# Two graph-attention and expert layers on one core: row norms written ahead of the mask step, and rows of x asked for on ScalarE's queue

## The chip, the cores and the metric

The kernel runs on one core of a Trainium2 chip. The metric is device time in microseconds (us). Beside it there is one profiled execution, whose trace gives every instruction of every engine: PE (TensorE, the matrix unit), ACT (ScalarE), DVE (VectorE), POOL (GpSimd) and SP (SyncE, which here does nothing but request transfers). "SPq" and "ACTq" in a row are the sequencers of those engines, and a DMA row there is the time in which the request is issued, not the time of the transfer.

## The reference, cut to what matters

The input is x (2708 rows of 256 float32) and an adjacency matrix adj (2708 x 2708, int32, about 1.2% ones). Four steps follow one another, each added to x:

```python
x = x + gnn0(layernorm(x), adj)      # q,k,v; softmax(q k^T / 16 where adj > 0) v; elu
x = x + ffn0(layernorm(x))           # 8 experts, the best 2 of each row, hidden 1024
x = x + gnn1(layernorm(x), adj)      # additive attention under the same mask
x = x + ffn1(layernorm(x))           # 8 experts, the best 2 of each row, hidden 512
```

Only the first of the four, and of it only the beginning, is touched by the change.

## The kernel before, in words

The 2708 rows are cut into NT = 22 tiles of up to 128 rows (the last has 20), and the queries into six blocks of 512 (the last has 148). `layer0_attention` runs over the blocks `b`, and inside a block over the 22 key tiles `k`. A step `k` of block `b` computes the scores of 512 queries against the 128 keys of tile `k` (`scores`, L586), takes the exponential (ACT, L598), multiplies it by the mask (DVE, L601), and three steps later (`LAG = 3`) `attend` adds the product with the values v to four accumulators (L650).

The first block does more than the others, since the keys and values do not exist yet. At step k of block 0 the tile k + 4 is prepared:

- `norm_begin` (bn_stats L282, bn_aggr L283, one more small DVE operation L284, a power on POOL L288), `norm_end` (L292, gives `xn`);
- `prepare`: two transposes on PE (L305), a copy of the result to `xnT` on ACT (L306), a sum on DVE (L499), the value matmuls on PE (L504, two of them, four passes), a copy to `v` on ACT (L508).

Tiles 0 to 3 are prepared ahead of the loop, tiles 4 to 21 in its steps 0 to 17. A tile of x is loaded by `load_x` (L408, 128 KB, into one of 9 buffers `xin`). Tiles 0 to 8 are asked for at the very start, tiles 9 to 21 in the steps 0 to 12, at step k the tile k + 9. Its buffer is the one that tile k had, which is free when `norm_end` of tile k has read it.

The masks come from adj. `masks_of(b)` is a generator that makes the mask of block `b` in pieces: five loads of 1 MB each (L425, four requests of 256 KB, into one of three buffers `adj`), and for each load four pairs of a comparison (`m_rows`, L446) and a 32x32 transpose (`mT`, L452) on DVE. Load i + 2 is written down right after the first comparison of load i. One `next(first_mask)` is one pair. In block 0 two such generators advance: `first_mask` for block 0 itself (its first three loads and its first four pairs are written ahead of the loop) and `later_mask` for block 1. A load into an `adj` buffer has to wait until the four comparisons of the load that had the buffer before are done.

What sets the order of the work:

- SP runs in the order of the program, everywhere (`tc.manual_schedule(engines={SP})` at the top). A request whose buffer is not free holds all requests behind it.
- In block 0, PE, ACT, DVE and POOL run in an order that a planner wrote down when the kernel was built. It simulates the machine with costs of its own, and of what is ready in its simulation it takes the operation that stands first in the program. On the chip each engine then keeps to that order, whatever arrives earlier or later there.
- From block 1 on (L689), PE, ACT and DVE run in the order of the program.

The other requests of SP in block 0 are `load_apart` (L464, at step 4), the packing of expert weights from a list called `background` (after step 8, on odd steps), and, from step 17, five `load_x` that bring the rows of block 0 back for its residual (these use the same function, with its default queue).

Of the kernel before, what the change touches and what calls it, by code (L numbers as in the profile page):

```python
# [27 lines left out]
NT = (N + P - 1) // P  # L28
ROWS = [min(P, N - t * P) for t in range(NT)]
# [14 lines left out]
def of_tile(rows, t):  # L44

    if t >= KEYS:
        return rows[t * P : t * P + ROWS[t], :]
    b = t // GROUP * BN
    return rows[b : b + BN, :].rearrange("(p j) d -> j p d", j=GROUP)[t % GROUP]
# [57 lines left out]
def adj_ffn_kernel(ctx: ExitStack, tc: tile.TileContext, a: dict, out: bass.AP):  # L107
    nc = tc.nc
# [168 lines left out]
    def norm_stats(src, r):  # L277

        st = small.tile([P, 6], F32, name="ln_st")
        mv = small.tile([P, 2], F32, name="ln_mv")  # L280
        rs = small.tile([P, 2, 2], F32, name="ln_rs")
        nc.vector.bn_stats(st[:r], src)  # L282
        nc.vector.bn_aggr(mv[:r], st[:r])  # L283
        nc.vector.scalar_tensor_tensor(  # L284
            rs[:r, 0], once_twice[:r, 0], mv[:r, 1:2], once_twice[:r, 1],
            op0=ALU.mult, op1=ALU.add,
        )
        nc.gpsimd.tensor_tensor(rs[:r, 1], rs[:r, 0], minus_half[:r], ALU.pow)  # L288
        return mv[:r, 0:1], rs[:r, 1, 0:1], rs[:r, 1, 1:2], rs[:r, 0, 0:1]

    def normed(dst, src, mean, factor):
        return nc.vector.tensor_scalar(dst, src, mean, factor, op0=ALU.subtract, op1=ALU.mult)  # L292
# [91 lines left out]
    def layer0_attention(line):  # L384
        with ExitStack() as scope, ExitStack() as until_last:
# [17 lines left out]
                return pool.tile(shape, dtype, name=f"{name}_last", bufs=bufs)  # L403
            xin = {}

            def load_x(t):
                xin[t] = rows0.tile([P, D], F32, name="xin", bufs=9)
                nc.sync.dma_start(xin[t][: ROWS[t]], of_tile(a["x"], t))  # L408

            def masks_of(b, of):  # L410

# [68 lines left out]
            def norm_begin(t):  # L480
                r, src = ROWS[t], xin.pop(t)
                return t, src, norm_stats(src[:r], r)

            def norm_end(t, src, stats):
                r, (mean, factor, *_) = ROWS[t], stats
                xn = rows.tile([P, D], F32, name="xn", bufs=4)
                normed(xn[:r], src[:r], mean, factor)
                return xn

            def prepare(t, xn):  # L490
                r = ROWS[t]
                at = xnT[:, :, t * P : t * P + r]
                if t < NT - 1:
                    to_columns(at, xn[:r], r)
                else:
                    tail_columns(x_tail, xn)
                    nc.vector.tensor_copy(at, x_tail[:, :, :r])
                    r, at = P, x_tail
                nc.vector.tensor_reduce(  # L499
                    sums_of[:, :, t], xnT[:, :, t * P : t * P + ROWS[t]], AX.X, ALU.add  # L500
                )
                ps = misc.tile([P, GROUP, P], F32, name="misc").rearrange("p g n -> p (g n)")
                for c in range(DC):
                    nc.tensor.matmul(  # L504
                        ps[:r, :D], at[:, c, :], wv[:, c, :],
                        start=(c == 0), stop=(c == DC - 1),
                    )
                nc.scalar.copy(v[:r, t, :D], ps[:r, :D])  # L508
# [3 lines left out]
            if True:  # L512
# [5 lines left out]
                for t in range(2, 9):  # L518
                    load_x(t)

                with tc.manual_schedule(
# [10 lines left out]
                    first_mask = masks_of(0, turned_of)  # L532
# [153 lines left out]
            for b, (b0, nb, ts_) in enumerate(BLOCKS):  # L686
                line.gap = GROUP if b >= last - 1 else GROUP + 1
                if b == 1:
                    order0.enter_context(  # L689
                        tc.manual_schedule(engines={  # L690
                            mybir.EngineType.PE,
                            mybir.EngineType.Activation,
                            mybir.EngineType.DVE,
                        })
                    )
                if b + 1 < len(BLOCKS):
                    turned_of[b + 1] = mask_of(b + 1)
                if b == 0:
                    later_mask = masks_of(1, turned_of)
                    next(later_mask)  # L700
                for k in range(NT):
                    if b == 0:
                        if k + 9 < NT:
                            load_x(k + 9)
                        next(first_mask, None)
                        if k + 4 < NT:
                            prepare(k + 4, norm_end(*norm_begin(k + 4)))

                    j = k - (2 if b == last else NT - 1 - GROUP)
                    if 0 <= j < len(ts_):  # L710
                        load_x(ts_[j])
                    if k == (0 if b == last else GROUP):
                        apart_adj = load_apart(b)
                    if k == NT - 8:
                        apart = compare_apart(*apart_adj)
                    late.append((b, k, scores(b, k, g, apart, mT)))
                    if len(late) > LAG:
                        b_, k_, p = late.pop(0)
                        if k_ == 0:
                            accs = [  # L720
                                ps_acc.tile([P, D + 1], F32, name="acc") for _ in BLOCKS[b_][2]
                            ]
                        attend(b_, k_, p, accs)
                        if k_ == NT - 1:
                            evict(b_, accs, total)
                    if b == 1 and k % 2 == 0:
                        next(folding, None)
                    if b == 0 and k == NT - 1:
                        sums = wide.tile([P, DC], F32, name="sums", bufs=1)
                        nc.vector.tensor_reduce(sums, sums_of, AX.X, ALU.add)  # L730
                        total = all_sum(wide, sums, wv, D, "total0")
                    if b == 0 and k == NT - 4:
                        raw = wide.tile([P, BN // QUARTER, P], I32, name="adj", bufs=3)
                        raw = raw.rearrange("p n e -> p (n e)").bitcast(F32)
                        nc.sync.dma_start(
                            raw, a["L0_ffn_Wr"].rearrange("d e -> (d e)").partition_broadcast(P)
                        )
                        gate_rows(raw)
                    if k == NT - 6 and b + 1 < len(BLOCKS):
                        g_next = queries(b + 1)  # L740
                    if k % 3 == 2 if b == last - 1 else k == 0 or k >= 2:
                        next(later_mask, None)
                    if k == NT - 3:
                        even_later = iter(())
                        if b + 2 < len(BLOCKS):
                            even_later = masks_of(b + 2, turned_of)
                            next(even_later)
                    if b > 0 and k == 2:
                        nc.sync.dma_start(neighbours[b - 1][:], turned_of[b - 1])
                    if background and k % 2 == 1 and b < last and (b > 0 or k > 8):  # L750
                        background.pop(0)()
                    if b > 0:
                        line.step()
                    if b == last and k == LAG:
                        until_last.close()
                    if b == last and k == LAG + 2:
                        n = FULL_AFTER[experts0.early]
                        guess0 = experts0.open(
                            [i * (n // RING) * E // (n + GROUP) for i in range(AHEAD)] + [-1]
                        )  # L760
                        for _ in range(AHEAD):
                            next(guess0)
                        begin0 = experts0.begin()
                    if b == last and LAG + 2 <= k < LAG + 8:
                        next(begin0)
                    if b == last and k in (LAG + 9, LAG + 13, LAG + 18):
                        next(begin0)
                if b == last:
                    nc.sync.dma_start(neighbours[b][:], mT)
                else:  # L770
                    for _ in later_mask:
                        pass
                    later_mask = even_later
                    g, mT = g_next, turned_of[b + 1]
# [1345 lines left out]
```

## Time and profile before

| what | value |
|---|---|
| device time, median of 3 runs | 1191.05 us (1186.0 to 1194.85) |
| the profiled execution: its own time, its span | 1177.48 us, 1175.8 us |
| granted TensorE clock in it, mean | 0.990 |
| PE, DVE, ACT, POOL busy in the span | 1125.0, 647.7, 415.4, 430.3 us |
| 0 to 20 us (weights folded, tiles 0 to 3, queries of block 0): PE busy, DMA share | 14.77 us, 0.96 |
| 20 to 132 us (block 0): PE, DVE, ACT busy, DMA share | 105.59, 64.67, 28.43 us, 0.74 |
| 132 to 212 us (block 1): PE, DVE, ACT busy, DMA share | 80.00, 62.07, 19.60 us, 0.75 |

The span is the time from the first to the last instruction in the trace; the execution's own time lies 1.7 us above it, and the median of the runs without a profile 13.6 us above that. A busy PE in such a table has matmuls in flight; it does not mean that the array starts a pass at every moment, so the starts of successive passes are the better measure of what a stretch of PE work costs. The rows of a timeline are: start, duration, engine, line, operation, out<-in, count, and in brackets the idle time of the engine ahead of it with what ended it.

### The profile page before, as it was taken

What the parts mean: (1) busy time and instruction counts of PE and PEld (TensorE: products, weight loads), DVE (VectorE), ACT (ScalarE), POOL (GpSimd) and SP (SyncE); (2) the same over time, 40 slices, a digit from 0 to 9 for tenths busy, and PEclk for the clock granted to TensorE, in tenths of its full rate; (3) what the DMA queues carried; (4) which work ended last, traced back from release to release, by engine and by line L of the source; (5) the groups of instructions that cost most, each with busy time, mean ns of one, the idle gap of its engine ahead of it and who ended that gap; (6) DMA issues with size and microseconds to landing.
All of it is one profiled execution on the core that took longest, in us unless ns stands there. A gap on an engine that the chain in (4) does not pass through costs nothing. (4 is left out here: it accounts for less than half of the span.)

```text
span 1175.8 us, 20858 instructions
## 1 busy us (share of the span) xinstructions
PE 1125.0 (96%) x6421; PEld 912.2 (78%) x6421; DVE 647.7 (55%) x2405; ACT 415.4 (35%) x1232; POOL 430.3 (37%) x519
## 2 busy tenths in 40 slices
PE   8989999999999999999999999998999998998993
PEld 5665666666666666789999999997899997898992
DVE  5565777786876867643222222222876777622224
ACT  3222222222222222433333333332777673344441
POOL 3001212121212122453434343423754557865552
PEclk9999999999999999999999999999999999999997
DMA  9678676867745658579675936543000517577346
GB/s 224 130 163 211 169 183 167 237 168 181 215 128 149 155 140 317 154 206 262 181 197 151 339 83 187 122 159 86 28 1 33 211 56 238 123 241 231 79 131 229
DMA packets 198661, 195.88 MB, mean 167 GB/s; under 512 B 90939, under 2 KB 181524, under 8 KB 192520
## 3 DMA queue, kind: packets, MB, share of 16 engines
q1 hardware_dynamic: 173242, 118.18, 39.7%
q0 software_dynamic: 24256, 70.81, 19.0%
q10 hardware_dynamic: 1038, 5.40, 1.3%
q8 instruction: 55, 0.90, 0.3%
q14 instruction: 70, 0.57, 0.2%
HBM read 246.19 MB, written 66.15 MB: 266 GB/s over the span
## 5 line engine op out<-in xcount | busy, mean ns | idle before, releaser
L1835 PEld LDWEIGHTS mm<-xe,ring 128*128 128x128 f32 x2192 | 260.6, 194 | 15.8 <-DVE xe L1808 5.8
L1835 PE MATMUL mm<-xe,ring 128*128 128x128 f32 x2192 | 263.9, 278 | 5.5 <-DVE xe L1808 3.9
L1843 ACT ACTIVATE hT<-mm,ring 128x128 f32<-128x128 f32 x548 | 156.6, 369 | 287.6 <-issue 157.2
L1851 PE MATMUL acc<-ring,hT 128*128 128x256 f32 x1096 | 252.1, 380 | 0.0
L1851 PEld LDWEIGHTS acc<-ring,hT 128*128 128x128 f32 x1096 | 201.6, 191 | 24.2 <-issue 0.4
L650 PEld LDWEIGHTS acc<-v,p 128*128 128x128 f32 (+1 forms) x880 | 160.0, 190 | 62.4 <-issue 37.0
L650 PE MATMUL acc<-v,p 128*128 128x257 f32 (+1 forms) x880 | 202.7, 383 | 0.0
L586 PE MATMUL s<-g,xnT 128*128 128x512 f32 x420 | 200.3, 597 | 0.6 <-DVE mT L605 0.6
L1551 POOL DMA_INDIRECT disp<-row,to x88 | 92.0, 1045 | 256.9 <-DVE x L670 125.5
L1857 DVE SCALAR_TENSOR_TENSOR y<-acc,who,bias 128x256 f32<-128x256 f32 x92 | 44.3, 481 | 254.6 <-PE acc L1851 232.9
L288 POOL TENSOR_TENSOR ln_rs<-ln_rs,minus_half 128x2 f32<-128x2 f32 x88 | 68.7, 782 | 172.9 <-DVE ln_rs L284 120.4
L598 ACT ACTIVATE p<-s 128x512 f32<-128x512 f32 x105 | 62.7, 597 | 194.8 <-PE s L586 178.7
L930 PE MATMUL acc<-parts,m 128*128 128x266 f32 x924 | 126.2, 293 | 0.0
L930 PEld LDWEIGHTS acc<-parts,m 128*128 128x128 f32 x924 | 117.1, 185 | 4.1 <-ACT raw L957 0.9
L586 PEld LDWEIGHTS s<-g,xnT 128*128 128x128 f32 x420 | 76.8, 190 | 55.1 <-issue 50.3
L1741 POOL DMA_INDIRECT ring<-L_ffn_packed,weight_row x76 | 80.2, 1055 | 92.4 <-PE acc L1851 61.8
L601 DVE SCALAR_TENSOR_TENSOR p<-p,mT 128x512 f32<-128x512 f32 x100 | 71.0, 710 | 75.3 <-ACT p L598 75.2
L1873 POOL DMA_INDIRECT xd<-y,who x45 | 71.2, 1583 | 111.3 <-DVE xe L1814 50.2
L897 ACT CAST m<-mT 128x512 fp32r<-128x512 fp8e4 (+4 forms) x168 | 71.8, 475 | 9.7 <-PE acc L930 6.3
L1863 POOL DMA_INDIRECT xd<-y,who x47 | 50.3, 1071 | 48.6 <-DVE y L1857 44.8
L272 DVE SCALAR_TENSOR_TENSOR row<-x,wr_rows 128x256 f32<-128x256 f32 x128 | 54.4, 425 | 3.3
L1814 DVE TENSOR_SCALAR xe<-xe_raw,ring 128x128 f32<-128x128 f32 x90 | 27.7, 352 | 40.2 <-DMA ring<-L_ffn_packed,weight_row 39.2
(337 smaller groups left out, 1073.1 us busy)
## 6 DMA issues: line engine op xcount, KB each, us to landing
adj<-in_adj_dram SPq DMA_DIRECT2D x100, 256.0 KB
L_ffn_packed<-in_L_ffn_W_dram SPq DMA_DIRECT2D x32, 512.0 KB
xg<-disp SPq DMA_DIRECT2D x368, 32.0 KB
L_ffn_packed<-in_L_ffn_W_dram SPq DMA_DIRECT2D x32, 256.0 KB
neighbours<-mT SPq DMA_DIRECT2D x5, 1408.0 KB
mT<-neighbours SPq DMA_DIRECT2D x5, 1408.0 KB
ring<-L_ffn_packed SPq DMA_DIRECT2D x3, 2182.0 KB
xin<-in_x_dram SPq DMA_DIRECT2D x42, 128.0 KB
```

Of the source, the lines that this page charges most:

```text
L288: nc.gpsimd.tensor_tensor(rs[:r, 1], rs[:r, 0], minus_half[:r], ALU.pow)
L586: nc.tensor.matmul(ps[:kr, :nb], xnT[:, c, k0 : k0 + kr], g[:, c, :nb], start=(c == 0), stop=(c == DC - 1 and k < KEYS),)
L601: nc.vector.scalar_tensor_tensor(p, p, LARGEST, mask, op0=ALU.min, op1=ALU.mult)
L650: nc.tensor.matmul(accs[j][:r], p[keys, q0 : q0 + r], v[keys, k, :], start=(k == 0), stop=(k == NT - 1),)
L897: nc.scalar.copy(m[:, : q1 - q0], MASKS[b].of_key(mTs[b], k)[:, q0 - b * BN : q1 - b * BN],)
L930: nc.tensor.matmul(acc[:r], masks[t], parts[:, k, i], start=(k == 0 and i == 0), stop=False,)
L1551: nc.gpsimd.indirect_dma_start(disp[:], bass.IndirectOffsetOnAxis(ap=to[:r, j : j + 1], axis=0), rows2[:r, j], None,)
L1741: nc.gpsimd.indirect_dma_start(w, None, packed[:], bass.IndirectOffsetOnAxis(ap=self.weight_row[:, s : s + 1], axis=0), bounds_check=E * P ...
L1835: nc.tensor.matmul(ps[:, i, :], w[:, c * hidden + f * P : c * hidden + (f + 1) * P], xe[:, c, :], start=(c == 0), stop=(c == DC - 1),)
L1843: nc.scalar.activation(hT[:, f, :], ps[:, i, :], AF.Gelu, bias=w[:, b1 + f : b1 + f + 1])
L1851: nc.tensor.matmul(ps, hT[:, f, :], w[:, w2 + f * D : w2 + (f + 1) * D], start=(f == 0), stop=(f == hc - 1),)
L1873: start = nc.gpsimd.indirect_dma_start(xd[:], at, y, None, bounds_check=N - 1, oob_is_err=False, compute_op=ALU.add)
```

## The change

In `load_x` the queue becomes an argument, with SP as its default. In block 0's loop three statements change places: `prepare` (with `norm_begin` and `norm_end` inside) now stands first, the load of tile k + 9 second and on ScalarE's queue, the step of the mask third.

```diff
-            def load_x(t):
+            def load_x(t, queue=nc.sync):
                 xin[t] = rows0.tile([P, D], F32, name="xin", bufs=9)
-                nc.sync.dma_start(xin[t][: ROWS[t]], of_tile(a["x"], t))
+                queue.dma_start(xin[t][: ROWS[t]], of_tile(a["x"], t))
...
                 for k in range(NT):
                     if b == 0:
-                        if k + 9 < NT:
-                            load_x(k + 9)
-                        next(first_mask, None)
                         if k + 4 < NT:
                             prepare(k + 4, norm_end(*norm_begin(k + 4)))
+                        if k + 9 < NT:
+                            load_x(k + 9, nc.scalar)
+                        next(first_mask, None)
```

No operation is added or removed: thirteen requests of 128 KB (the last of 20 KB) go from SP to ACT, and the planner sees another order of the program in block 0.

## The prediction

> **What bounds the kernel now.** I began with the busy time of the engines in stretches. PE is busy for 1125.0 of 1175.8 us, and from 132 us on (block 1) for 80.00 of 80.00 us, so the attention is bound by PE. In block 0 it is not quite. What a step costs when nothing is missing is seen in the timeline of 28 to 45 us:
>
> ```profile
> 38.21 1.88 PE L586 MATMUL s<-g,xnT 128*128 128x512 f32 x4
> ...
> 39.93 1.90 PE L650 MATMUL acc<-v,p 128*128 128x257 f32 x8
> ...
> 41.66 1.88 PE L586 MATMUL s<-g,xnT 128*128 128x512 f32 x4
> ```
>
> Read the starts, not the durations: four score passes take 1.72 us (0.43 each), eight attend passes 1.73 us (0.216 each). In the same way two transposes take 0.21 us and the four value passes of a tile 0.87. Multiplied by the counts that the groups of instructions give for 16.5 to 135.1 us (100 score passes, 168 attend passes, 70 value passes, 16 passes for queries at 0.43, 34 transposes, and 4.7 us of small ones) this is 43.0 + 36.3 + 15.1 + 6.9 + 3.7 + 4.7 = 109.7 us of work in a stretch of 118.6. **PE loses 8.9 us there.** The same rates over block 1 (135.1 to 214.5 us) give 79.8 us of work in 79.4, so the rates are good to half a microsecond and block 1 loses nothing.
>
> Where block 0 loses shows in the waits of PE in 20 to 132 us (total, times, longest):
>
> ```profile
> PE misc L305 <- DVE ln_rs L284: 3.2, 2, 2.2
> PE misc L504 <- ACT xnT L306: 1.8, 4, 0.5
> PE misc L305 <- DVE ln_mv L283: 0.7, 1, 0.7
> PE s L586 <- DVE mT L605: 0.6, 1, 0.6
> ```
>
> Three of the four belong to the preparation of a tile: PE has nothing left but the transposes of a tile that is not normed (3.9 us), or two tiles follow one another so closely that it waits for the copy between transposes and value matmuls (1.8).
>
> Then I asked why tiles are late, in SP's timeline:
>
> ```profile
> 24.07 2.58 SPq L425 DMA_DIRECT2D adj<-in_adj_dram  x4
> 26.69 0.61 SPq L408 DMA_DIRECT2D xin<-in_x_dram  x1
> 35.61 8.83 SPq L425 DMA_DIRECT2D adj<-in_adj_dram  x8
> 44.49 1.09 SPq L408 DMA_DIRECT2D xin<-in_x_dram  x2
> 52.22 2.58 SPq L425 DMA_DIRECT2D adj<-in_adj_dram  x4
> 54.84 1.09 SPq L408 DMA_DIRECT2D xin<-in_x_dram  x2
> 62.76 2.58 SPq L425 DMA_DIRECT2D adj<-in_adj_dram  x4
> 65.39 0.63 SPq L464 DMA_DIRECT2D adj_rest<-in_adj_dram  x1
> 66.06 1.09 SPq L408 DMA_DIRECT2D xin<-in_x_dram  x2
> ```
>
> Tile 9 is asked for at 26.69, tile 10 only at 44.49, because two loads of adj stand between them and wait for a buffer. Each row of x leaves in the shadow of a mask load. And the order of DVE was written by a planner that reckoned with this. Tiles 14 and 15 are requested at 66.06, but their statistics come at 81.12:
>
> ```profile
> 81.12 0.73 DVE L282 BATCH_NORM_STATS2 ln_st<-xin 128x6 f32<-128x256 f32 x2
> ...
> 83.67 0.41 PE L305 MATMUL misc<-ident,xn 128*128 128x128 f32 x2 [2.17 <-DVE ln_rs L284]
> ```
>
> DVE waits for xin only once in the kernel (3.8 us at the very start), so the rows had landed; they stand behind a mask product of step 13 and three comparisons in DVE's order. That is the 2.17 us wait.
>
> **The change part by part.**
>
> *Thirteen requests leave SP.* At the median of 0.43 us (tile xin, L408) SP is spared 13 x 0.43 = 5.6 us. Nothing on PE's path waits for SP's issuing itself, so this alone is worth nothing. The mask loads behind them don't go out 5.6 us earlier either: L425 waits for DVE 21.6 us behind mT L452 and 7.1 behind m_rows L446 in that stretch, that is for a buffer.
>
> *The rows come early.* Tile k + 9 needs only the buffer of tile k. Tiles 0 to 3 are normed by 11.5 us, 4 to 8 by 21, so with a free queue tiles 9 to 17 can be asked for by about 21 us instead of 26.69 to 70, and the last well before 45. Here a rule speaks against the change: the Trainium skill, "DMA: Bandwidth & Descriptors", section "Issuing engines are not separate DMA queues", says that requests from several engines end on the same 16 DMA engines and that a second issuing engine saves only the issue time, usually small. By the rule the gain is those 5.6 us of a sequencer that isn't the bound: 0, and 1191. By SP's rows what is saved isn't issue but the hold of 17.8 us between tile 9 and tile 10. I go by the rows, as the rule leaves out a queue standing at a semaphore. Where it does hold is bandwidth: 13 x 128 KB = 1.7 MB move into a stretch (5 to 30 us) where the DMA share is already 0.9 to 1.25; at the 220 GB/s seen there, loads of adj land up to 7.6 us later. The second load of block 0 is compared from 30.77 us, and by the bytes moved until then it had landed near 19, so that cover holds.
>
> *The norms stand first.* In the planner's order of preference the statistics, the norm and the transposes of tile k + 4 now come ahead of that step's comparison, and their rows are there. PE should find a normed tile at each step and place its transposes between score passes, as at 20 to 31 us, where a whole round of scores and preparation takes 2.94 us for 2.80 of work. I take the 3.9 us of waits for a norm as gone. Of the 1.8 us behind the copy I take half: 0.9. The remaining loss (0.6 behind L605, which is the 3.87 us reduction L262, and about 2.6 of small gaps) stays. Gain: 4.8 us; bounds 0 (the planner makes other gaps) and 8.9.
>
> *The comparisons stand later.* Each pair is 0.42 + 0.42 us on DVE, which is busy 64.67 of 112 us; a pair is put back by at most the operations of one tile, 0.41 + 0.17 + 0.22 + 0.41 + 0.41 = 1.6 us. The first key whose mask could be missed is the first of a load (12, 16). The fourth load of adj is asked for from 35.61 us, and the first mask product that needs it (L601 of step 12) runs at 76.99. Cost 0; if the cover is gone, 1.6 us for each of the two loads.
>
> *Thirteen requests on ACT.* No row of before has ACT asking in this stretch; the nearest are ACT's own ring loads, 0.34 us (L1887), and SP's xin, 0.43. I take 0.43: 5.6 us of ACT, which is busy 28.43 of 112. Queued behind a request are the copies L306 (PE waits for them: 9.1 us of weight loads held in 15 times) and the exponentials (three steps of slack). A request hurts only in the window around a copy, about 0.7 + 0.43 of a 4.6 us step: 5.6 x 0.25 = 1.4, less where the planner puts them into ACT's gaps: I take 0.8. Bounds 0 and 5.6, and 11.7 if each is held as SP's first twelve adj requests were (10.77 us, 0.9 each).
>
> **Sum**: -4.8 + 0.8 = -4.0 us, 1177.48 to 1173.5 for an execution like the profiled one. The runs without a profile lie 13.6 us higher at the median, and I carry the difference over: 1191.05 - 4.0 = **1187.0**. Block 1 and what follows keep their order, PE is all but full up to 461 us, so a gain in block 0 arrives whole.
>
> **The rivals.**
>
> *ScalarE is held by its own requests (slower).* For it: SP's queue shows that a request can stand for 8.8 us; the same page, section "Anatomy of one DMA", has every semaphore wait happen on the issuing sequencer before dispatch, and SP's waits agree (21.6 us behind DVE). On SP nothing but requests stood behind; on ACT the copies and exponentials do. If the order written at build time puts requests where, on the chip, the buffer's norm or an older transfer is late, PE pays. Place: 8 to 45 us. It decides from the point where the holds beside a copy exceed the 4.8 us gained. At 0.9 us each, 11.7; if early rows also make the planner set tiles in a row without scores between (two at 71.33 to 75.08 take 3.75 us for some 3.0 of work, 0.35 a tile), another 13 x 0.35 = 4.5. If no wait is removed either: 1191 + 16 = **1207**; with half of both **1199**. Against it: the buffers in question are free early.
>
> *Hidden anyway.* The planner's order moves the gaps, PE waits for masks instead of norms, and the sum stays: **1191**. For it: the loads of adj keep their order and their buffers, and block 0 needs ten of them, 10.5 MB. Against it: no matmul waits for a mask product now, and weight loads do for 1.0 us only.
>
> *More than the norms.* All 8.9 us go, and the 5.2 us that PE idles in 0 to 20 too: **1177**. Against it: the first 20 us hang on weights and copies that don't change.
>
> **How the numbers follow.** 1% of this kernel is 12 us, about what a measurement can tell from no change. Forecast 0.43, slower 0.33, hidden 0.14, more 0.10. The forecast's own range, 1182 to 1191, lies within 1%. Faster by over 1% (under 1179) needs more than PE's whole loss in block 0: 0.10, the last rival. Slower by over 1% (over 1203) gets two thirds of the first rival, 0.22, since an order rewritten by a planner has no firm bound from the profile; the rest, 0.68, is within 1%. The range, 1180 to 1207, holds the forecast, the hidden case and the first rival up to its full price, and leaves out the last and what lies above.
>
> **What would show it.** Right: xin requests of tiles 9 to 17 on ACTq before 25 us; the wait of PE L305 for ln_rs gone; block 1 beginning some 4 us earlier; the same PE counts. Wrong: ACTq rows of several us, PE L504 waiting more behind xnT, or PE L650 waiting for DVE p: then order or masks, not rows, set block 0.

## The result, and the profile after

The changed kernel is a little slower: 1193.45 us (median of 20 runs) against 1188.05 us (20 runs of the kernel before on the same chip), **ratio 1.0047 with an interval of 1.0032 to 1.0062**, some 5.6 us. Forecast were 4 us less. The profiled execution of after has a span of 1192.1 us at a granted clock of 0.984 (before 1175.8 at 0.990), so the ends of these two executions say little about the change. The attention says more: from 212 to 425 us PE is busy for 211.44 us in both, and the difference lies ahead of that.

Three starts on PE locate the loss: the first query pass (L570, end of the prologue), the first pass of the gate (L226, just behind block 0's last attend) and the last query pass of the attention.

| | before | after | difference |
|---|---|---|---|
| first query pass, L570 | 16.6 us | 20.9 us | +4.3 |
| first gate pass, L226 | 132.4 | 136.5 | +4.1 |
| last query pass, L570 | 422.1 | 428.5 | +6.4 |

So 4.3 us are lost ahead of the queries, where the prediction expected nothing, 0.2 are gained in block 0, where it expected 4.0, and 2.3 are lost in block 1, where it expected nothing. Up to the last of these marks PE is granted its full clock in both executions wherever the trace records it.

**Ahead of the queries.** The timeline of after (start, duration, engine, line, operation, count, and in brackets the idle time ahead of it with what ended it), 4 to 12 us:

```profile
4.31 0.80 ACT L545 COPY mT<-misc 128x256 f32<-128x256 f32 x2 [2.23 <-PE misc L544]
...
7.63 0.46 DVE L292 TENSOR_SCALAR xn<-xin,ln_mv,ln_rs 128x256 f32<-128x256 f32 x1
...
8.11 0.39 ACTq L408 DMA_DIRECT2D xin<-in_x_dram  x1
...
8.55 0.65 ACT L545 COPY mT<-misc 128x256 f32<-128x256 f32 x2 [3.44 <-DMA xin<-in_x_dram]
...
8.98 3.36 PE L550 MATMUL s<-mT 128*128 128x256 f32 x7 [3.01 <-ACT mT L545]
```

The four copies L545 belong to the folding of the weights; PE can't go on without them. The planner has set ScalarE's first request of x between the second and the third, and ScalarE stands there from 5.11 to 8.11 us. The request itself takes 0.39 us: what costs is not its row but the idle time in the row behind it. Before, the third copy started at 5.45 us:

```profile
5.45 0.80 ACT L545 COPY mT<-misc 128x256 f32<-128x256 f32 x2 [0.35 <-PE misc L544]
```

Of the 4.3 us the hold itself is 3.1 (the first pass of L550 starts at 8.98 instead of 5.87 us). The other 1.2 is PE's pace: from there to the queries PE takes 11.9 instead of 10.7 us. The trace's record of the clock begins, at full, only at 13.7 us instead of 8.1, and the eight passes L550 start 0.43 us apart after the first, where before they did so up to 8.15 us and then followed at 0.21. Three more requests stand in the prologue, at 9.24, 10.73 and 11.73 us. Each goes out 0.02 to 0.03 us after a norm L292 has let go of its buffer: the norms of tiles 1, 2 and 3 end at 9.21, 10.71 and 11.70 us.

**In block 0** the waits of PE in 20 to 132 us (total, times, longest), to be laid beside those of before:

```profile
PE acc L650 <- DVE p L601: 2.3, 2, 2.0
PE misc L504 <- ACT xnT L306: 1.4, 3, 0.5
PE s L586 <- DVE mT L605: 1.2, 1, 1.2
PE misc L504 <- ACT x_tail L350: 0.7, 1, 0.7
PE misc L570 <- ACT v L508: 0.4, 1, 0.4
```

The waits for a norm are gone, all 3.9 us, as forecast. In their place PE waits for masked scores, for the reduction behind mT and for copies: 6.0 us in all against 6.3. DVE's timeline tells why. Between these two rows it makes, after one mask product, only the norms and sums of tile after tile, and not one comparison:

```profile
37.58 0.42 DVE L446 TENSOR_SCALAR m_rows<-adj 128x512 fp8e4<-128x512 int32 x1
...
65.03 0.75 DVE L446 TENSOR_SCALAR m_rows<-adj 128x512 fp8e4<-128x512 int32 x2
```

By 65 us 20 of the 22 tiles are normed (before: 12), and afterwards PE lives on masks; DVE makes no comparison from 69.9 to 93.3 us either. The attends come in bursts of 32 passes, and at 96.29 us one waits 1.99 us for its mask.

SP is late as well. Its waits in 0 to 60 us have two new lines (before had none for xin there):

```profile
SPq L425 <- DMA xin<-in_x_dram: 14.0, 5, 6.2
SPq L536 <- DMA xin<-in_x_dram: 6.6, 3, 2.9
```

SP asks for adj and constants here, and yet stands until rows of x land; all but 0.9 us of it are rows that ScalarE asked for. The records of the requests tell why (the trace holds them, the views leave this part out). Each request names a semaphore that its transfer raises on landing, and does not go out before the earlier transfer with the same semaphore has landed. SP's and ScalarE's requests share the eight numbers 101 to 108. The request of adj at 24.57 us, for instance, waits for 108 and takes 108; ScalarE's row of 22.39 us had that number before, and SP has stood since 18.33, for 6.2 us, and for the first 4 of them ScalarE had not even asked. It works the other way round too: ScalarE's first request takes 107 from a row that SP asked for at 3.77 us, which landed at 7.66, and only then waits for its norm.

The fourth load of adj goes out at 42.2 instead of 24.1 us. The fifth, at 65.8 instead of 35.6, has stood 21.5 us for the late comparisons and transposes (mT L452).

**In block 1** what stood at the end of SP's queue comes too late:

```profile
131.78 0.59 SPq L214 DMA_DIRECT2D wdst_b<-in_L_gnn_w_att_dram  x1
...
139.39 0.42 DVE L217 SCALAR_TENSOR_TENSOR junk<-wfc,wdst_b 128x256 f32<-128x256 f32 x1 [5.92 <-DMA wdst_b<-in_L_gnn_w_att_dram]
...
141.89 1.57 PE L650 MATMUL acc<-v,p 128*128 128x257 f32 x6 [2.04 <-DVE raw L676]
```

wdst_b, a vector for the second attention's gate, is asked for at 131.8 instead of 108.3 us. From block 1 on DVE keeps the order of the program: its eviction of block 0 (raw, L676) stands behind L217, and PE needs the accumulators that it frees.

### The profile page after: what moved, and what is told of

Same layout as the page of the kernel before. It is cut to its first block, busy times and chain, and to the rows that moved or that the text cites. A ratio compares the mean times of both kernels' runs of the same rounds, so it can differ in the third digit from the quotient of the medians.

```text
span 1192.1 us, 20863 instructions
## 1 busy us (share of the span) xinstructions
PE 1132.3 (95%) x6421; PEld 917.4 (77%) x6421; DVE 643.7 (54%) x2405; ACT 413.1 (35%) x1232; POOL 429.0 (36%) x519
## 5 line engine op out<-in xcount | busy, mean ns | idle before, releaser
L1851 PE MATMUL acc<-ring,hT 128*128 128x256 f32 x1096 | 254.9, 383 | 0.0
L650 PEld LDWEIGHTS acc<-v,p 128*128 128x128 f32 (+1 forms) x880 | 159.9, 190 | 65.6 <-issue 35.8
L650 PE MATMUL acc<-v,p 128*128 128x257 f32 (+1 forms) x880 | 201.9, 383 | 4.3 <-DVE p L601 2.3
L930 PE MATMUL acc<-parts,m 128*128 128x266 f32 x924 | 126.2, 293 | 0.0
L601 DVE SCALAR_TENSOR_TENSOR p<-p,mT 128x512 f32<-128x512 f32 x100 | 68.1, 686 | 46.6 <-ACT p L598 46.5
```

Source lines behind the costliest of these rows:

```text
L601: nc.vector.scalar_tensor_tensor(p, p, LARGEST, mask, op0=ALU.min, op1=ALU.mult)
L650: nc.tensor.matmul(accs[j][:r], p[keys, q0 : q0 + r], v[keys, k, :], start=(k == 0), stop=(k == NT - 1),)
L930: nc.tensor.matmul(acc[:r], masks[t], parts[:, k, i], start=(k == 0 and i == 0), stop=False,)
L1851: nc.tensor.matmul(ps, hT[:, f, :], w[:, w2 + f * D : w2 + (f + 1) * D], start=(f == 0), stop=(f == hc - 1),)
```

## The experiments

All ratios are against the kernel before, run on the same chip, with 95% intervals. The three marks are those above, of one profiled execution each. The last column is the time ahead of the last query for which that execution was granted half the clock; PE moves at half pace there, so at most half of that time is to be taken off the last mark (an estimate).

| run | first query | L226 | last query | ratio | half clock, us |
|---|---|---|---|---|---|
| e1 order only | 16.5 | 132.4 | 422.1 | 1.0002 (0.9989 to 1.0015) | 0 |
| e2 queue only | 19.9 | 135.3 | 428.8 | 1.0064 (1.0041 to 1.0087) | 3.4 |
| e10 one request on ScalarE | 20.0 | 138.8 | 428.5 | 1.0043 (1.0028 to 1.0059) | 6.8 |
| e4 ACT in program order | 17.1 | 132.4 | 426.5 | 1.0011 (0.9997 to 1.0026) | 10.2 |
| e3 rows on GpSimd's queue | 17.2 | 131.9 | 426.9 | 1.0054 (1.0032 to 1.0075) | 3.4 |
| e6 after, wdst_b early | 20.7 | 136.0 | 428.4 | 1.0056 (1.0035 to 1.0076) | 0 |
| e7 e4, wdst_b early | 17.6 | 133.3 | 425.7 | 0.9995 (0.9980 to 1.0010) | 6.8 |
| e9 e7 in the old order | 17.3 | 130.2 | 422.6 | 0.9989 (0.9976 to 1.0003) | 3.4 |
| e14 e7, gate rows early | 16.4 | 130.9 | 421.6 | 0.9991 (0.9979 to 1.0002) | 0 |
| e16 e6, gate rows early | 22.4 | 139.1 | 429.8 | 1.0054 (1.0034 to 1.0074) | 0 |
| e5 four rows ahead on SP | 17.1 | 130.6 | 421.8 | 0.9981 (0.9971 to 0.9992) | 0 |
| e11 e5, wdst_b early | 17.2 | 130.5 | 423.0 | 0.9995 (0.9984 to 1.0006) | 0 |
| e13 e5, mask step first | 16.8 | 131.3 | 422.5 | 1.0006 (0.9990 to 1.0022) | 0 |
| e12 only tiles 9 to 12 early, SP | 17.0 | 139.4 | 429.1 | 1.0044 (1.0029 to 1.0058) | 6.8 |
| e15 e11, gate rows early | 17.0 | 140.7 | 431.4 | 1.0059 (1.0037 to 1.0081) | 10.2 |
| **e17 tiles 9 to 12 on SP, rest on ScalarE** | 17.1 | 126.2 | 415.8 | **0.9932 (0.9909 to 0.9954)** | 0 |
| e18 e17 in the old order | 16.9 | 126.0 | 415.6 | 0.9934 (0.9913 to 0.9955) | 0 |
| e19 tiles 9 to 14 on SP | 17.1 | 129.4 | 419.0 | 0.9962 (0.9949 to 0.9976) | 0 |

### Which edit, and which request: e1, e2, e10

e1 keeps the new order and gives the rows back to SP:

```diff
-                            load_x(k + 9, nc.scalar)
+                            load_x(k + 9)
```

> The three statements in the new order, but the 13 rows of x asked for on SP as before. Ratio to the kernel before (the whole change measured 1.0047, +5.4 us). If the hold of ScalarE ahead of the first queries (3.4 us of ACT, queries 4.3 us later) is the cause: ACT asks for nothing, queries start again at 16.6 us, 1.000 to 1.001. If the order is the cause (masks late in the order of DVE, attends in bursts): about +4 us, 1.003 to 1.004, with PE L650 waiting for DVE p L601 by some 2 us. If the gain of the prediction was real and comes from the order alone: 0.997.

e2 keeps the old order and changes the queue alone:

> The old order of the statements, but the 13 rows asked for on ScalarE's queue. If the hold of ScalarE ahead of the first queries is the cause, it is here too: ACT idle 3 us or more before 10 us, queries from about 20.9 instead of 16.6 us, and the ratio 1.003 to 1.005; if besides the early rows save the norm waits of block 0 (3.9 us), these cancel it: 1.000. If the order is the cause, this kernel has none of it: 1.000 or below, 0.997 with the norm waits gone.

e10 is the kernel before with a single request moved:

```diff
-                            load_x(k + 9)
+                            load_x(k + 9, nc.scalar if k == 0 else nc.sync)
```

> The kernel before, with one request of thirteen moved: tile 9 on ScalarE's queue, tiles 10 to 21 on SP, the statements in their old order. The planner sets it between the second and the third of the four copies of the folded weights (L545); it needs the buffer of tile 0, whose norm (DVE L292) ends at 8.1 us. If the hold ahead of the queries is the work of that one request: ACT idles some 3.4 us until 8.5, queries start about 3 to 4 us later than at 16.6, and the ratio is 1.0025 to 1.0035. If it takes all four requests of tiles 9 to 12 ahead of the queries (each at the norm of its buffer, 8.1, 9.2, 10.7, 11.7 us): PE gets back most of it while it waits for weights, 1.000 to 1.001.

Measured: the order of the statements does nothing, and PE's waits in block 0 stay those of before to the tenth; e1's first row reads

```profile
PE misc L305 <- DVE ln_rs L284: 3.2, 2, 2.2
```

As long as the rows come late, the preference for preparation has nothing to prefer. The queue alone has the whole loss, with the same hold (3.0 us of ScalarE), the same mask waits (2.3 us) and the same wait in block 1 (1.9 us). And one request of the thirteen is enough for 3.4 us ahead of the queries (e10, 4 to 10 us):

```profile
7.28 0.41 DVE L292 TENSOR_SCALAR xn<-xin,ln_mv,ln_rs 128x256 f32<-128x256 f32 x1
8.06 0.40 ACTq L408 DMA_DIRECT2D xin<-in_x_dram  x1
...
8.51 0.65 ACT L545 COPY mT<-misc 128x256 f32<-128x256 f32 x2 [3.39 <-DMA xin<-in_x_dram]
```

Here the norm of tile 0 has let go of the buffer at 7.69 us and the request still stands until 8.06, so for this first one the landing of an earlier row is the last thing waited for, as the bracket says; in the changed kernel the norm came last (8.09, request 8.11). Both end within 0.4 us of one another, so both would have to go to free ScalarE. Of e10's 1.0043 (5.1 us, 3.3 to 7.0) 3.4 are ahead of the queries; the rest is not explained. In its profiled execution another 3.0 us are lost between the query and L226, where PE's waits in 20 to 132 us are line for line those of before; it was granted half its clock for 6.8 us (columns: busy us of PE, PEld, DVE, ACT, POOL, then the clock, DMA share, GB/s):

```profile
86.90:93.70 6.80, 6.18 (x14) 4.04 (x15) 2.25 (x8) 1.12 (x3) 0.74 (x1) 0.50 1.14 281
```

That is 3.4 us of PE's pace at most. The stretch begins at the end of a 2.17 us wait for a norm that the kernel before has as well (at 81.5 us), there with the clock at full, so these 3.0 us are not put down to the request.

### Taking the hold away: e4, e3

e4 keeps ScalarE's queue but has ScalarE run block 0's loop in the order of the program, so that no request can stand ahead of the queries:

```diff
+            act_order = ExitStack()
+            act_order.enter_context(
+                tc.manual_schedule(engines={mybir.EngineType.Activation})
+            )
...
                 if b == 1:
+                    act_order.close()
```

> The changed kernel, but in block 0's loop ACT runs in the order of the program, so that no request of x can stand ahead of the copies of the folded weights: the first one comes after the queries of block 0. If the hold ahead of the first queries is the cause: queries at 16.6 us again, -4.3 us against the changed kernel, ratio 1.000 to 1.001; ACT may in exchange hold exponentials and copies in a fixed order, which costs PE waits for xnT and p of a few us at most. If the order of the masks or the late request of the second attention's weights is the cause: no better than 1.004.

e3 is the changed kernel with `nc.gpsimd` in place of `nc.scalar`.

> The changed kernel with the 13 rows asked for on GpSimd's queue. If requests on ACT hold ACT and hold those of SP behind them: ACT idles no 3.4 us before 10 us, SP's first twelve requests of adj go out in some 11 us again instead of 24.9, queries start near 16.6 us; ratio about 1.000, 0.997 if the norm waits are gone for good. POOL's own powers (L288) can then be late behind a request: up to 13 x 1 us of POOL, of which PE would see a part as waits of L305 for ln_rs. If the order of the masks is the cause: 1.003 to 1.004 as with ScalarE's queue.

In both the queries start about where they did (17.1 and 17.2 us), which is 3.7 of the 4.3 us. In e4 the time follows: 1.0011 is not clear of no change, where the changed kernel has 1.0047. Its last mark of 426.5 us seems to say otherwise, but holds 10.2 us at half clock, worth up to 5.1. This row shows the first of them, a wait and behind it 31 passes in 10.0 us, where 32 take 7.1 at full clock:

```profile
64.28 10.01 PE L650 MATMUL acc<-v,p 128*128 128x257 f32 x31 [2.80 <-DVE p L601]
```

In e3 the time does not follow (1.0054), though its half clock explains at most 1.7 of the 4.8 us at the last query. What else is lost has moved on: e4's waits of PE in 20 to 132 and in 132 to 215 us are

```profile
PE acc L650 <- DVE p L601: 3.7, 2, 2.8
```

```profile
PE acc L650 <- DVE raw L676: 2.5, 1, 2.5
```

The masks alone now take what the norms took. e3 has 1.9 us of the first kind and 3.4 of the second. In e3 the waits of SP for xin are 0.3 us in 0 to 60 us, in e4 20.7: SP stands behind ScalarE's requests of x and not behind GpSimd's, whose records have semaphores of their own, 110 to 117. But the comparisons are late in e3 too (none between 40.7 and 60.7 us), and its fifth load of adj goes out at 61.4 us: for the late masks SP's hold isn't needed, the planner's order is enough. Nor does the order of the three statements set it: e2, in the old order, has the same pause (36.6 to 63.7 us).

### The end of SP's queue: e6, e7, e9, e14, e16

In e6 and e7 wdst_b is asked for ahead of block 0's loop (a `yield` behind the request in `fold_gate`, and a first `next(folding)` ahead of the loop). e9 is e7 with the three statements in their old order.

> The changed kernel, with one request moved: wdst_b (128 KB, the vector of the second attention's gate) is asked for ahead of block 0's loop instead of in block 1. If PE's wait of 2.0 us for raw L676 in block 1 comes from DVE standing 5.9 us at wdst_b, both go and the ratio falls from 1.0047 by 0.0017 to 1.003; the 4.3 us ahead of the queries stay. If the wait is only the shadow of something else that is late in block 1 (loads of adj, x): no change, 1.0047.

> The changed kernel with ACT in the order of the program in block 0's loop and wdst_b asked for early. Theory of two prices (hold ahead of the queries 4.3 us, wdst_b 2.0 to 2.5 us, against a gain in block 0): with both taken away the gain of block 0 is left; ACT in program order alone measured 1.0011 with 2.5 us of PE waiting in block 1, so 0.999 here, and block 0 from the first query pass to L226 of block 1 some 1 to 4 us shorter than the 115.8 us of before. If early rows gain nothing in block 0 (masks wait in place of norms): 1.000 or above.

> The same as the kernel before it (ACT in program order, wdst_b early), but with the three statements in their old order: request of x, mask step, preparation. The order alone measured 1.0002 while rows were late; if it decides nothing also where rows are early: the same ratio within 0.001. If with early rows the preparation ahead of the mask step is what makes masks late (3.7 us of PE L650 waiting for DVE p): this one is better by up to 3 us, 0.997, with those waits gone.

The wait for raw goes, and in its place stand two others. e6 and e7 both show them in block 1 (lines are one higher there):

```profile
PE s L587 <- ACT p L599: 1.4, 1, 1.4
PE misc L571 <- ACT g L575: 0.8, 1, 0.8
```

Behind the first is the reduction of the gate's rows (3.85 us of DVE): its load sits in SP's queue among the late loads of adj, so the reduction starts at 134.99 us in block 1 (e7), where DVE's order is fixed, instead of 118.5 in block 0. So e14 and e16 write these rows at step 10 instead of step 18:

```diff
-                    if b == 0 and k == NT - 4:
+                    if b == 0 and k == 10:
```

> The changed kernel with ACT in program order and wdst_b early (0.9995), and the gate's rows (the load into an adj buffer, reduction L263, product L265) written at step 10 of block 0 instead of step 18. If the wait left in block 1 (1.4 us for ACT p, 0.8 for g) is the reduction standing in DVE's fixed order there: it ends in block 0, both waits go, queries of block 2 start about 2 us earlier than the 186.6 us of the kernel without this edit, ratio 0.998. If the load waits for its adj buffer all the same, or DVE pays 3.8 us in block 0 instead: 0.9995 or above.

> The changed kernel with wdst_b and the gate's rows early, ScalarE's requests where the planner put them. Theory of two prices: the hold ahead of the queries stays (queries at 20.9 us), the 2 us of block 1 go: queries of block 2 near 188 us instead of 190.4, ratio 1.003 to 1.0035. If the second block's loss has another cause: 1.0047 to 1.0056 as before.

From L226 to the last query e6 and e7 take 292.4 us, e14 and e16 290.7, before 289.7: 1.7 us come back, 1.1 stay, of which 0.8 with g. The end of SP's queue is thus the cause of most of block 1's loss, as a chain of two late loads, of which either alone is enough. In the whole time it doesn't show (e16 1.0054 against 1.0056 of e6; e14 against e7 is within the intervals), and the marks tell where it went: e16 takes 116.7 us in block 0 where e6 takes 115.3, with one more wait of 1.46 us for a mask product, which stands behind the reduction there (e14 has the same wait). Its queries at 22.4 us are pace again: the record of its clock begins at 18.2 us, that of e6 at 13.5.

Where ScalarE is not held ahead of the queries, block 0 does show the forecast's gain: less the half clock, e7 and e9 take an estimated 112.7 and 111.2 us from the first query to L226 instead of 115.8. Block 1 takes 2.7 us of it back, and the ratios (0.9995, 0.9989) are not clear of no change. The old order of the statements (e9) changes nothing beyond the intervals, with early rows as with late ones.

### Rows early without ScalarE: e5, e11, e13, e12, e15

e5 asks for tiles 9 to 12 on SP right behind the first twelve adj requests and for tile k + 13 in step k, with the three statements in the new order; none of these requests is ScalarE's.

```diff
+                for t in range(9, 13):      # behind the first twelve adj requests
+                    load_x(t)
...
+                        if k + 13 < NT:
+                            load_x(k + 13)
```

> No request on ScalarE: tiles 9 to 12 are asked for on SP right behind the first twelve adj requests, and step k asks for tile k + 13 on SP behind the preparation of tile k + 4, ahead of the mask step. If the cost of the whole change is that of ScalarE's queue alone (its hold ahead of the queries, 4.3 us), early rows on SP give the forecast's gain: ratio 0.997. If early rows by themselves set masks and loads of adj back (PE L650 waiting for DVE p L601 in block 0, wdst_b asked for late and PE waiting for raw L676 in block 1 by 2 to 3.4 us, as in the kernels with rows on ACT and on POOL): 1.001 to 1.003, since each SP request of x now stands at the norm of a tile of the same step and holds adj behind it.

> Rows four tiles further ahead on SP (which measured 0.9981) with wdst_b asked for ahead of block 0's loop. If the 1.3 us that PE waits for raw L678 in block 1 are those of wdst_b: 0.997. If, as in the changed kernel, the reduction L263 of the gate's rows then stands in the same place (3.85 us of DVE in block 1 in program order): no gain, 0.998.

> Rows four tiles further ahead on SP, with the mask step ahead of preparation and request in each step. If the order of the statements decides once rows are early (preparation first leaves DVE without a comparison from 32 to 54 us and sets adj loads back by 20 us): comparisons come earlier, the fifth load of adj goes out near 36 instead of 55 us, wdst_b near 108 instead of after 120, the wait for raw L678 is gone, ratio 0.996 to 0.997. If the order decides nothing, as with late rows (1.0002): 0.998.

e12 is the kernel before with only tiles 9 to 12 moved so, and e15 is e11 with the gate's rows at step 10.

> The kernel before, with only tiles 9 to 12 asked for earlier (on SP, right behind the first twelve adj requests), and tiles 13 to 21 where they were. If rows further ahead gain by removing norm waits wherever they come early: a part of the 0.0019 that all rows gave, 0.999, with the waits of L305 for tiles 14 and 15 (2.2 us at 83.7) still there. If the gain hangs on the later tiles (13 to 21) being asked for four steps earlier: 1.000.

> Rows four tiles ahead on SP, wdst_b early (0.9995) and the gate's rows at step 10. If the end of SP's queue costs the second block its 1.6 and 0.8 us: queries of block 2 at 181.5 us instead of 183.9 (before: 184.0), ratio 0.997. If not: 0.9995, and what rows ahead of time can give is nothing that this can measure.

e5, e11 and e13 end block 0 by 1.2 to 2.0 us earlier than before, and give it back in block 1; at the last query they stand at -0.3, +0.9 and +0.4 us. e5's 0.9981 is more than its marks explain, and neither e11 nor e13 repeats it: I count the three as no change. e12 was expected at 0.999 and came out at 1.0044. With four early tiles the preparation of these runs ahead, no comparison starts from 32.3 to 54.4 us, and then the tiles behind them are as late as ever (tile 13 is asked for at 71.2 us, before at 55.5): PE pays for both, and its profiled execution also has two stretches of 3.4 us at half clock, one at each of these waits.

```profile
70.76 8.68 PE L652 MATMUL acc<-v,p 128*128 128x257 f32 x32 [3.35 <-DVE p L603]
...
88.92 0.41 PE L305 MATMUL misc<-ident,xn 128*128 128x128 f32 x2 [2.23 <-DVE ln_rs L284]
```

e15 found a trap. Its early rows set POOL's product of the gate's rows ahead of the last tile's small power (POOL's timeline), and PE waits 7.4 us for the norm behind that power (L346 is the tail's transpose), with 10.2 us at half clock from 114.5 us on:

```profile
112.55 6.00 POOL L265 TENSOR_TENSOR wr_rows<-adj,gate_mean 128x2048 f32<-128x2048 f32 x1 [6.21 <-DVE gate_mean L264]
118.49 0.68 POOL L289 TENSOR_TENSOR ln_rs<-ln_rs,minus_half 20x2 f32<-20x2 f32 x1
```

### Leaving the first four on SP: e17, e18, e19

```diff
-                            load_x(k + 9, nc.scalar)
+                            load_x(k + 9, nc.scalar if k >= 4 else nc.sync)
```

> The changed kernel, with tiles 9 to 12 left on SP and tiles 13 to 21 on ScalarE. In ScalarE's order no request stands ahead of the queries now; the nine follow one another behind the second query copy and some exponentials. If the 4.3 us hang on the requests whose buffers are still being normed: queries at 16.6 us again. Then nine in a row hold ScalarE in block 0 as long as the last buffer's norm is late, and exponentials behind them: at 1 us each 9 us of ScalarE near 40 to 60 us, of which PE may pay 2 to 5; ratio 1.000 to 1.004. If the cost were one per request on ScalarE: two thirds of 1.0047, 1.003, with queries late as well.

> Tiles 9 to 12 on SP and 13 to 21 on ScalarE (0.9932), with the three statements in their old order. ScalarE's, POOL's and SP's orders are then the same as in that kernel, only DVE's and PE's differ in places. If the order decides nothing, as with late rows (1.0002) and with ScalarE in program order (0.9989 against 0.9995): 0.993. If the preparation ahead of the mask step is what removes the norm waits: 0.996 to 0.997, with PE L305 waiting for ln_rs again.

> The changed kernel with tiles 9 to 14 left on SP and 15 to 21 on ScalarE. If the gain is that of rows the planner takes as early, with no request ahead of the queries: queries at 17 us, the norm waits of tiles 14 and 15 (2.2 us) back in part since tile 14 is late again, ratio 0.994 to 0.996. If the 0.9932 is the luck of one order: 0.998 to 1.004.

**This version beats both kernels**, 0.9932 and, in a set of runs of its own with the old order (e18), 0.9934: about 8 us. The hold ahead of the queries is gone, and with it every wait of PE in block 0 but one. All that PE waits for in e17 from 20 to 132 us is

```profile
PE misc L504 <- ACT xnT L306: 0.9, 2, 0.5
```

and the windows of e17 (columns as above) have PE busy for 111.06 of 112 us where before had 105.59, and full in block 1:

```profile
20.00:132.00 112.00, 111.06 (x442) 73.65 (x441) 70.68 (x197) 30.32 (x69) 15.58 (x16) 1.00 0.76 167
132.00:212.00 80.00, 80.00 (x319) 52.17 (x318) 62.02 (x232) 19.32 (x45) 12.46 (x18) 1.00 0.86 216
```

The nine requests hold ScalarE longer than the first one of the changed kernel did (6.56 against 3.44 us), and cost next to nothing, since PE has 32 attend passes in hand for just that time. These rows are from two timelines, of PE and of ACT:

```profile
65.10 7.10 PE L650 MATMUL acc<-v,p 128*128 128x257 f32 x32
72.04 0.38 PE L305 MATMUL misc<-ident,xn 128*128 128x128 f32 x2
```

```profile
65.36 5.17 ACTq L408 DMA_DIRECT2D xin<-in_x_dram  x9
72.46 0.37 ACT L306 COPY xnT<-misc 128x256 f32<-128x256 f32 x1 [6.56 <-DMA xin<-in_x_dram]
```

Nor do the rows come much earlier than before: tiles 13 to 21 go out from 65.4 to 70.0 us, before from 55.5 to 85.0. What changed is the order that the planner wrote with them in view: from 71.0 to 85.1 us the norms of tiles 13 to 21 follow one another, each with its score passes, and the comparisons that go with the first tiles stay where they were (fifth load of adj at 36.1 us, wdst_b at 110.3). e18 has it in the old order of the statements as well. e19, with two fewer on ScalarE, has half the gain and the expected wait back:

```profile
PE misc L305 <- DVE ln_rs L284: 2.3, 1, 2.3
```

So the gain of e17 isn't tied to one lucky order, but it is an order's gain: it was found in e17 by looking for the cause, and its size (6.3 us at the last query, against an expected 0 or a loss) was not foreseen. Why the planner writes this order for nine moved requests, and the other for thirteen, is not shown: its simulation is not on record.

## Why the prediction was wrong

- **What bounds the kernel, and the 8.9 us lost in block 0: right.** e17 takes 109.1 us from the first query to L226 instead of 115.8, 6.8 of the 8.9.
- **The rows come early, the waits for L305 go: right in the sign, wrong in what follows.** In the changed kernel tiles 9 to 17 went out from 8.1 to 26.8 us, near the forecast 21, and the 3.9 us of norm waits went. But the gain of 4.8 did not come: block 0 took 115.6 us instead of 115.8. Where ScalarE runs in program order it did come, an estimated 3.1 to 4.6 us (e7, e9), and was lost again in block 1.
- **"The comparisons stand later. Cost 0": the step that failed in block 0.** A comparison was not put back "by at most the operations of one tile", 1.6 us: none started for 27 us, where before the longest pause up to 113 us was 10: the planner had put the norms of the later tiles ahead, not only of the one. That it does so because their rows are there in its simulation fits its rule, but is not shown. The mask waits (2.3 us), the reduction behind mT (0.6 more) and two copies (1.1) took the place of the norms. This is the mechanism of the rival "hidden anyway".
- **"Thirteen requests on ACT", +0.8 us: the step that failed by size and place.** It sought the price in a window around the copies of block 0. The requests stood in the prologue, one between the weight copies, and the queries came 4.3 us later (3.1 the hold, 1.2 PE's pace behind it), inside the bounds of 0 to 5.6 and five times the value taken. The rival "ScalarE is held by its own requests" had this mechanism, with 8 to 45 us as the place; it happened from 5 to 12. Its counter-argument, "the buffers in question are free early", fails for just the first four tiles: early is 8.1 to 11.7 us, and ScalarE was needed at 5.45.
- **"Block 1 and what follows keep their order, so a gain in block 0 arrives whole": failed by 2.3 us.** SP's lateness ended in block 1. The prediction had adj land "up to 7.6 us later" by bandwidth; SP was held at landings of xin for 20.6 us instead, by semaphores that it shares with ScalarE.
- **The order edit** was given most of the gain; alone it is worth nothing (1.0002), and beside the queue edit nothing (0.9932 and 0.9934).
- **The rule weighed in the prediction**, the Trainium skill, "DMA: Bandwidth & Descriptors", "Issuing engines are not separate DMA queues": a second issuing engine saves only issue time. By it the change is worth 0, by the rows of SP 4.8 us. No run decides between them: e17 gains 6.3 us, but its rows go out hardly earlier than before, so the gain is the order's, and the changed kernel loses 6.4. The rule leaves out what a second queue costs the engine that it belongs to.
- **"ACTq rows of several us" as the mark of failure** was the wrong thing to look for: the rows stayed at 0.33 to 0.55 us. The hold shows as idle time of the next ACT row. The other mark, PE L650 waiting for p, did appear.
- **Two readings are off, without weight in the sum.** The load of adj asked for at 35.61 us is the fifth; the fourth, which step 12 needs, leaves at 24.07, so the cover was longer than stated. And four comparisons, not three, stand ahead of the statistics at 81.12 us.

Sum of the account: +4.3 ahead of the queries, -0.2 in block 0, +2.3 in block 1, 6.4 us in the profiled execution; the runs give 5.6 (3.8 to 7.4).

Still open: why the planner puts the comparisons off, what e3 loses beyond its marks (1.0054 is 6.4 us, its last mark less the half clock about 3.1), and how often the half-clock stretches fall into block 0 in executions without a profile.

## What to carry to other kernels

A request moved to a computing engine's queue costs what stands behind it there, not its issue time: look where the planner puts it, and if its buffer or an older transfer is still busy at that moment, keep that request on the queue of an engine that does nothing else. Look also at which semaphore it shares: two queues that take their semaphores from one set are not independent. Here four requests of thirteen turned a gain of 8 us into a loss of 5.6; of the 12.7 us between the two last marks 3.8 lie ahead of the queries, 6.6 in block 0 and 2.3 in block 1. And when work is made ready earlier, ask what the planner will now put off for it: PE lives on two suppliers, norms and masks, and spending the one early leaves it to wait for the other.

## What was not expected of the hardware

- ScalarE and SP are tied through their transfers in this program: SP's requests of adj and constants waited 20.6 us (in 0 to 60 us) for rows of x, all but 0.9 for rows that ScalarE had asked for, at the eight semaphores that both use; with the rows on GpSimd's queue, which has eight others, it was 0.3 us.
- A small DVE operation can last as long as a large one on POOL beside it. In e7 the operation L330 (128x1, median 0.16 us over 22) took 4.08 us and ended with POOL's product:

```profile
139.12 4.91 POOL L265 TENSOR_TENSOR wr_rows<-adj,gate_mean 128x2048 f32<-128x2048 f32 x1 [56.43 <-DVE gate_mean L264]
...
139.97 4.08 DVE L330 SCALAR_TENSOR_TENSOR z<-alone,raw 128x1 f32<-128x1 f32 x1
```

- PE's clock is granted at half for stretches of 3.4 us and multiples of it. The profiled executions of before, after, e1, e5, e6, e11, e13, e14, e16, e17, e18 and e19 have none in the first 200 us, those of e2, e3, e4, e7, e9, e10, e12 and e15 one or two between 63 and 145 us (3.4 to 10.2 us in all), which moves their marks by up to 1.7 to 5.1 us. Each of these ten stretches begins during a wait of PE of 1.9 to 7.4 us or at most 2.0 us behind it, as in e2 (PE idle from 138.6 to 140.5 us, half clock from 141.7). Waits as long pass without one too, 2.2 us in before and 3.3 in e14, so what decides is not shown; but a wait of PE can cost more than its own length, and e17, which has no wait over 0.5 us in blocks 0 and 1, shows none there. A mark of a single execution is to be read with its clock beside it.
